# A fused Mamba and mixture-of-experts layer on one core: more identity products at the start, one mixer product ahead of the router's, one small step on another engine, and a new planned order

## The chip, the cores and the metric

The kernel runs on one core of a Trainium2 chip. The core has five engines with a queue of instructions each: TensorE (PE, matrix products; its weight loads are shown as PEld), VectorE (DVE), ScalarE (ACT), GpSimd (POOL) and SyncE (SP, which here only starts DMA transfers). Each engine takes its own instructions strictly in the order in which the program lists them; between engines semaphores pass the word that something is done. The metric is the device time of one execution in microseconds. Before the change three executions took 1305.14, 1308.02 and 1309.28 us, with a median of 1308.02 us.

## The reference

The input x has 16 batches of 256 positions and 256 features, all in float32. Each batch is normalised (layer norm without weights) and goes through two branches, whose results are added to x.

```python
def _L0_attn_ref(input_states, W_in, conv_kernel, conv_bias, W_x, W_dt, b_dt, W_out, A_log, D):
    proj = jnp.einsum('blh,he->bel', input_states, W_in)       # 256 -> 2 x 512 features
    hidden, gate = jnp.split(proj, 2, axis=1)
    x = lax.conv_general_dilated(hidden, conv_kernel, ...)     # 4 taps along the positions
    hidden = jax.nn.silu(x + conv_bias[None, :, None])
    hs_ble = hidden.transpose(0, 2, 1)
    ssm_p = jnp.einsum('ble,ed->bld', hs_ble, W_x)
    dt, Bm, Cm = jnp.split(ssm_p, [TR, TR + N], axis=-1)       # 128, 16, 16
    dts = jax.nn.softplus(jnp.einsum('blr,re->ble', dt, W_dt) + b_dt)
    dA = jnp.exp(dts[..., None] * A[None, None])               # 512 features x 16 states
    dBu = dts[..., None] * Bm[:, :, None, :] * hs_ble[..., None]
    ...                                                        # state = dA * state + dBu, y = sum over n of state * C
    y = (scan_out + hidden * D[None, :, None]) * jax.nn.silu(gate)
    return jnp.einsum('bel,eh->blh', y, W_out)

def _L0_ffn_ref(hidden_states, router_w, w_gate, w_up, w_down):
    probs = jax.nn.softmax(x @ router_w.T)                     # 32 experts
    rw, sel = jax.lax.top_k(probs, 8)                          # 8 of them kept, weights normalised
    ...                                                        # per expert e: acc += w_e * ((silu(x @ wg) * (x @ wu)) @ wd)

x = x + _L0_attn_ref(xn, ...) + _L0_ffn_ref(xn, ...)
```

All 32 experts (96 inner features each, 3072 together) are computed for every position; an expert that was not chosen has weight zero.

## The kernel before, in words

**Tiles and work of one batch.** A batch's x is loaded as one tile `xt` (`load_x`, L250). VectorE takes mean and variance (`stats`, L357), ScalarE the root (`root`, L367), VectorE the reciprocal (`invert`, L372), GpSimd the product minus mean times reciprocal in two tiny instructions (`center`, L378), and ScalarE normalises in place (`norm`, L385). TensorE turns the result (`turn`, L393), ScalarE copies it out of the accumulator memory as `xnT` (`keep_turned`, L401). Everything after that reads `xnT`:

- The router: `route` (L406) multiplies by the router's weights, VectorE, ScalarE and VectorE again make the eight largest weights (`largest`, `expo`, `choose`), SP writes them to DRAM (`send_weights`, L456, four transfers), and `spread` (L467, six transfers for each quarter of the experts) reads them back repeated over the partitions as `wr`, in a ring of two buffers.
- The experts, in 12 pairs q of column blocks: `gates` (two pairs at once, tiles pg), `silu` (tiles sg, ring of three), `weigh` on GpSimd (sg times wr, L509), `ups` (tiles pu), `combine` on VectorE (h = pu times sg, L513, ring of two), `down` (acc grows by h times the down weights, L525).
- The mixer: `project` (L531, two halves q of two column blocks, tiles ph), the convolution as `conv_first` on ScalarE (L542) and three taps `conv_rest` on VectorE (L554), `activate`, then `params`, `keep_params`, `send_params` (B and C to DRAM as bcd) and `widen`, `steps` (the step sizes dts), `skip`, `inputs`. The scan runs in 8 groups g of two states: `fetch` reads B and C of a group back over all partitions (tile rep, ring of three, L637), `feed` on GpSimd makes B times u (tile bu, L649), `decay` on ScalarE exponentiates (da, L663), `scan` and `read` on VectorE (L671, L683), and `collect` lets a DMA of GpSimd's queue add the product to y (L688). At the end `gate`, `gate_silu`, `fold`, `gated`, `project_out`, `finish`, `settle`, `store`.

**What sets the order.** The order on every engine is written by a planner at build time (class `Plan`, L20): each step is given an engine, a planned length, a due time, what it needs, and which slots of buffer rings it takes and gives back. `Plan.order` plays the steps through, and whenever an engine is free it takes the ready step with the earliest due time whose rings have room. The due time of a step is a base time of its batch (ORIGIN plus the batch's number times PERIOD, or RATE for the experts) plus an offset by kind of step from the tables DUE, and for the first, second and last batch also from FIRST, SECOND and LAST (`add`, L770). `early` holds a step back until its due time minus that. The planner's result is only an order: on the chip the engines run freely along it.

**DMA.** SP starts all loads from its one queue, in order. ScalarE's queue starts five small loads (`small`, L266 to L274) at the beginning. These transfers share eight completion semaphores, numbered 0 to 7, in rotation: a transfer that comes to a semaphore again first waits until the transfer before it on that semaphore has landed. The five small loads hold numbers 0 (conv kernel), 2 (conv bias), 4, 6 and 7, so SP's first three loads hold 1, 3 and 5, and from its fourth on SP goes through 0, 1, 2 and so on. In the order before, SP's first loads are x, router weights, first half of W_in, then W_x (number 0), W_dt (1), x again for the residual (2), and the first quarter of the expert weights.

**The start.** `warm` (L347) lets TensorE turn the identity 14 times from the moment it exists, `keep_warm` (L352) 6 times more after the router's weights were turned, and 4 times after the first `turn`.

Of the kernel before, what the change touches and what calls it, by code (L numbers as in the profile page):

```python
# [13 lines left out]
ALU = mybir.AluOpType  # L14
# [106 lines left out]
def mamba_moe_kernel(  # L121
# [30 lines left out]
    nc = tc.nc  # L152
# [26 lines left out]
    ORIGIN = -7.2  # L179
    PERIOD = 79.1  # L180
    RATE = 79.0

    DUE = dict(
        load_x=-300.5, stats=-15.5, root=132.5, invert=-162.0, center=-75.0, norm=244.0,
        turn=-535.0, keep_turned=-94.0, route=-100.0, largest=-231.5, expo=221.0, choose=-1192.5,
        send_weights=-260.5, project=-51.5, conv_first=455.5, conv_rest=185.0, activate=-293.5,
        params=-209.0, keep_params=-266.0, send_params=-303.5, widen=-273.0, steps=-79.0,
        skip=120.0, inputs=-299.5, fetch=-252.5, feed=315.5, decay=-34.0, scan=539.0, read=55.9,
        collect=-257.0, spread=65.5, gates=-25.5, ups=669.0, silu=245.5, weigh=233.0,
        combine=-138.5, down=288.0, settle=-496.5, gate=50.5, gate_silu=216.0, fold=502.5,  # L190
        gated=894.5, project_out=-81.0, load_again=-68.0, finish=160.0,
    )
    EARLY = dict(
        load_x=175.0, load_experts=25.0, stats=37.0, turn=1.0, route=277.0, project=671.0,
# [3 lines left out]
        route=179.5, largest=36.5, expo=-163.5, choose=655.5, project=409.0, conv_first=-563.0,  # L198
        conv_rest=-561.0, activate=218.5, params=-266.5, keep_params=285.0, widen=-51.5,
        steps=971.5, skip=-377.0, inputs=295.0, fetch=-161.5, feed=-360.0, decay=-135.0, scan=36.5,  # L200
        read=33.0, collect=-157.0, spread=-263.5, gates=-97.5, ups=-247.0, silu=-204.0,
        weigh=270.0, combine=402.0, down=53.0,
# [3 lines left out]
        load_x=-132.5, stats=-1.0, root=-131.0, invert=-137.5, center=-86.0, norm=251.0,  # L206
        turn=267.0, keep_turned=-305.5, route=89.0, largest=-27.5, expo=-14.0, choose=46.0,
        send_weights=8.0, project=267.5, conv_first=36.5, conv_rest=-36.5, activate=-61.0,
        params=26.0, keep_params=178.5, send_params=13.0, widen=126.5, steps=-25.0, skip=225.5,
        inputs=-138.5, fetch=-56.0, feed=24.0, decay=7.0, scan=104.0, read=31.5, collect=-154.0,  # L210
        spread=8.0, gates=1.5, ups=-251.0, silu=46.5, weigh=-137.5, combine=48.0, down=100.5,
        settle=-112.0, gate=-10.0, gate_silu=-83.0, fold=99.0, gated=-152.0, project_out=-44.0,
        load_again=-35.0, finish=22.5,
# [3 lines left out]
        fetch=-123.0, feed=-25.0, decay=359.0, scan=571.0, read=-65.0, collect=-281.5,  # L217
        spread=-131.0, gates=216.5, ups=75.5, silu=445.0, weigh=-274.5, combine=448.0, down=296.5,
        settle=-10.0, gate=-75.5, gate_silu=105.5, fold=-115.5, gated=339.0, project_out=-460.5,
        finish=479.0,  # L220
    )
    LEAD = -28.0
# [14 lines left out]
        rep=3, bu=3, pr=4, da=AHEAD, g=2, u=2, acc=1, wr=2, sg=3, h=2, gs=2, o=1,  # L237
# [140 lines left out]
    def center(b):  # L378
        mv, rstd = live["st", b]
        nmr = p1.tile([P, SPS, 1], F32, tag="nmr", name=f"nmr_{b}")  # L380
        nc.gpsimd.tensor_mul(nmr, mv[:, :, 0:1], rstd)
        nc.gpsimd.tensor_scalar(nmr, nmr, -1.0, None, ALU.mult)
        live["st", b] = rstd, nmr
# [382 lines left out]
    b = 0  # L766
    MM = 0.432
    KB = 1 / 280

    def add(kind, key, engine, length, due, *args, early=None, **kw):  # L770
        fn = kw.pop("fn", None) or steps_of[kind]
        if early is None:
            early = EARLY.get(kind, 1e9)
        due += DUE.get(kind, 0.0) + (FIRST.get(kind, 0.0) if b == 0 else 0.0)
        due += SECOND.get(kind, 0.0) if b == 1 else 0.0
        due += LAST.get(kind, 0.0) if b == B - 1 else 0.0
        plan.add((kind, *key), engine, length, due, fn, *args, early=early, **kw)

    steps_of = dict(
        load_x=load_x, stats=stats, root=root, invert=invert, norm=norm, turn=turn,  # L780
        keep_turned=keep_turned, route=route, largest=largest, expo=expo, choose=choose,
        project=project, conv_first=conv_first, conv_rest=conv_rest, activate=activate,
        params=params, keep_params=keep_params, widen=widen, steps=steps, skip=skip, inputs=inputs,
        fetch=fetch, spread=spread, gates=gates, ups=expand, silu=silu, combine=combine,
        weigh=weigh, down=down, settle=settle, gate=gate, gate_silu=gate_silu, gated=gated,
# [7 lines left out]
    add("keep_warm", (1,), "PE", 1.3, -490.0, 6, needs=[("turn_router",)])  # L793
    add("keep_warm", (2,), "PE", 0.8, -490.0, 4, needs=[("turn", 0)], gives=["warm"])
# [12 lines left out]
    for b in range(B):  # L807
        t = ORIGIN + PERIOD * b
        last = [] if b else [("load_in", 0)]
        x = ("x", b)  # L810
# [7 lines left out]
        add("center", (b,), "POOL", 0.15, t, b, needs=[("invert", b)], gives=[("mv", b)])  # L818
# [3 lines left out]
        add("turn", (b,), "PE", 1.0, t, b, needs=[("norm", b)], gives=[x],  # L822
# [3 lines left out]
        add("route", (b,), "PE", 0.9, t if b else t + 30.0, b, needs=[("keep_turned", b), ("keep_router",)],  # L826
# [4 lines left out]
        add("choose", (b,), "DVE", 1.35, t, b, needs=[("expo", b)], gives=[("pl", b)])  # L831
# [3 lines left out]
        for q in range(2):  # L835
            add("project", (b, q), "PE", 4 * MM, t, b, q, needs=[("keep_turned", b)] + last + ([("project", b, 0)] if q else []),
                takes=[("gu"[q], ("ph", b, q))] + ([] if q else [("hs", hs)]), gives=[xT])
            add("conv_first", (b, q), "ACT", 0.92, t, b, q, gives=[("ph", b, q)],
                needs=[("project", b, q)] + ([("conv_first", b, 0)] if q else []))
            add("conv_rest", (b, q), "DVE", 2.4, t, b, q,  # L840
                needs=[("conv_first", b, q)], gives=[("ph", b, q)])
# [20 lines left out]
        for g in range(GROUPS):  # L862
            at = t + PERIOD / GROUPS * g
            add("fetch", (b, g), "SP", 512 * KB, at, b, g, needs=[("send_params", b)],
                takes=[("rep", ("rep", b, g))], lands=5.5, early=14.0)
# [32 lines left out]
        for i in range(PARTS):  # L898
            add("spread", (b, i), "SP", 3.0, e + RATE / PARTS * i, b, i,
                needs=[("send_weights", b)], takes=[("wr", ("wr", b, i))], lands=6.0, early=20.0)  # L900
        for i in range(PAIRS // BATCH):
# [21 lines left out]
        add("load_again", (b,), "SP", 256 * KB, t, b, takes=[("o", ("o", b))], lands=8.0, early=25.0)  # L923
# [5 lines left out]
            needs=[("keep_turned", b)] + ([] if b else [("load_in", 1)]), early=10.0)  # L929
# [10 lines left out]
        for q in range(PAIRED):  # L940
# [8 lines left out]
            lands=7.0)  # L949
# [33 lines left out]
```

## Time and profile before

| what | value |
|---|---|
| times of three executions | 1305.14, 1308.02, 1309.28 us |
| the profiled execution, span | 1309.5 us, mean granted TensorE clock 0.993 |
| PE busy | 1288.9 us (98%), 5978 matrix instructions |
| PEld busy | 1109.9 us (85%) |
| DVE, ACT, POOL busy | 1157.5 (88%), 1133.9 (87%), 1181.6 us (90%) |
| DMA | 268.80 MB, mean 205 GB/s |
| chain of work that ended last | PE 63%, POOL 12%, DVE 8%, issue 6%, DMA 5%, ACT 4% |
| instructions by row | warm 128x128 transposes x24; ACT_TABLE_LOAD 1283 ns each; weigh (L509) x192, mean 1922 ns; feed (L649) x256, mean 2924 ns |

The times of the table are those of one profiled execution of 1309.5 us, 1.5 us above the median of the three timed ones. A busy TensorE is not the same as a TensorE at its full pace, because matrix instructions are pipelined and their ends are modelled; how many of them fall into a stretch tells more. All five engines are busy for 85% and more, so an instruction that one engine takes late is soon felt by the others.

### The profile page before, as it was taken

What the parts mean: (1) busy time and instruction counts of PE and PEld (TensorE: products, weight loads), DVE (VectorE), ACT (ScalarE), POOL (GpSimd) and SP (SyncE); (2) the same over time, 40 slices, a digit from 0 to 9 for tenths busy, and PEclk for the clock granted to TensorE, in tenths of its full rate; (3) what the DMA queues carried; (4) which work ended last, traced back from release to release, by engine and by line L of the source; (5) the groups of instructions that cost most, each with busy time, mean ns of one, the idle gap of its engine ahead of it and who ended that gap; (6) DMA issues with size and microseconds to landing.
All of it is one profiled execution on the core that took longest, in us unless ns stands there. A gap on an engine that the chain in (4) does not pass through costs nothing.

```text
span 1309.5 us, 18902 instructions
## 1 busy us (share of the span) xinstructions
PE 1288.9 (98%) x5978; PEld 1109.9 (85%) x5978; DVE 1157.5 (88%) x1719; ACT 1133.9 (87%) x1898; POOL 1181.6 (90%) x835
## 2 busy tenths in 40 slices
PE   9979999999999999999999999999999999999998
PEld 7868888887888888888888888888888888888887
DVE  3778989999899998989899898898989899899986
ACT  5878898997989989899898989989899898998883
POOL 1778999999999989999999898999999989998995
PEclk8999999999999999999999999999999999999999
DMA  9998899899999989999998988989899989998994
GB/s 248 241 230 191 189 237 195 215 206 211 201 222 198 226 199 200 199 212 206 199 215 188 213 191 206 225 189 209 185 216 216 197 193 203 217 210 193 202 221 94
DMA packets 169940, 268.80 MB, mean 205 GB/s; under 512 B 37840, under 2 KB 103920, under 8 KB 169840
## 3 DMA queue, kind: packets, MB, share of 16 engines
q0 software_dynamic: 36576, 124.80, 50.4%
q1 hardware_dynamic: 130624, 142.75, 40.4%
q8 instruction: 47, 0.77, 0.2%
q10 hardware_dynamic: 2640, 0.05, 0.1%
q14 instruction: 53, 0.43, 0.1%
HBM read 137.51 MB, written 5.24 MB: 109 GB/s over the span
## 4 chain that ended last, share of the span: by engine, by line
PE 63%; POOL 12%; DVE 8%; issue 6%; DMA 5%; ACT 4%; SPq 1%; POOLq 0%; DVEq 0%; ACTq 0%
PE acc L525 16%; PE pg L490 16%; PE pu L490 16%; POOL bu L649 6%; POOL sg L509 4%; PE px L574 3%; PE po L742 3%; PE ph L536 3%; DVE da L671 3%; PE pgate L716 3%; DMA y<-pr 2%; POOL y L688 2%; DVE hs L559 2%; DVE pr L683 2%; ACT da L663 2%
## 5 line engine op out<-in xcount | busy, mean ns | idle before, releaser
L649 POOL TENSOR_TENSOR bu<-rep,hs 128x1024 f32<-128x1024 f32 x256 | 716.4, 2924 | 59.7 <-DMA rep<-bcd 34.2
L671 DVE TENSOR_TENSOR_SCAN da<-da,bu 128x512 f32<-128x512 f32 x512 | 609.0, 1217 | 53.0 <-ACT da L663 44.8
L663 ACT ACTIVATE da<-dts,a_sb 128x256 f32<-128x256 f32 x1024 | 469.6, 473 | 84.6 <-DVE pr L683 61.9
L490 PE MATMUL pu<-xnT,wu_sb 128*128 128x256 f32 x1536 | 362.5, 382 | 5.8 <-DVE h L513 5.5
L525 PE MATMUL acc<-wd_sb,h 128*128 128x256 f32 x1536 | 364.2, 380 | 3.9 <-DVE h L513 3.8
L490 PE MATMUL pg<-xnT,wg_sb 128*128 128x256 f32 x1536 | 348.8, 380 | 3.1 <-DVE hs L559 1.5
L490 PEld LDWEIGHTS pu<-xnT,wu_sb 128*128 128x128 f32 x1536 | 292.6, 191 | 48.0 <-DVE h L513 7.5
L490 PEld LDWEIGHTS pg<-xnT,wg_sb 128*128 128x128 f32 x1536 | 291.0, 190 | 46.1 <-ACT sg L503 2.9
L525 PEld LDWEIGHTS acc<-wd_sb,h 128*128 128x128 f32 x1536 | 291.6, 190 | 45.1 <-DVE h L513 5.1
L509 POOL TENSOR_TENSOR sg<-sg,wr 128x512 f32<-128x512 f32 x192 | 326.3, 1922 | 2.3 <-ACT sg L503 2.3
L688 POOL DMA_DIRECT2D y<-pr x222 | 299.9, 1352 | 16.6 <-DVE da L671 5.8
L683 DVE TENSOR_TENSOR pr<-da,rep 128x512 f32<-128x512 f32 x448 | 294.0, 676 | 2.7 <-DVE pr L683 0.7
L663 ACT ACT_TABLE_LOAD x151 | 193.7, 1283 | 2.6
L513 DVE TENSOR_TENSOR h<-pu,sg 128x512 f32<-128x512 f32 x192 | 131.1, 683 | 58.9 <-POOL sg L509 31.8
L503 ACT ACTIVATE sg<-pg 128x512 f32<-128x512 f32 x192 | 105.3, 594 | 4.3 <-PE pg L490 2.1
L503 ACT ACT_TABLE_LOAD x81 | 103.9, 1283 | 2.9 <-PE pg L490 1.5
L732 POOL TENSOR_TENSOR y<-y,gs 128x512 f32<-128x512 f32 x30 | 79.4, 2816 | 0.2
L559 DVE SCALAR_TENSOR_TENSOR hs<-ph,small,hs 128x255 f32<-128x255 f32 (+2 forms) x192 | 76.0, 471 | 1.9 <-ACT hs L548 1.9
L707 POOL TENSOR_TENSOR y<-y 128x512 f32<-128x512 f32 x32 | 64.6, 2347 | 0.5 <-DMA y<-pr 0.5
L536 PE MATMUL ph<-xnT,win_sb 128*128 128x256 f32 x256 | 63.4, 392 | 0.0
L742 PE MATMUL po<-wout_sb,y 128*128 128x256 f32 x256 | 60.8, 380 | 1.0 <-DVE hs L559 1.0
L574 PE MATMUL px<-hs,wx_sb 128*32 128x256 f32 (+1 forms) x256 | 61.4, 387 | 0.0
(66 smaller groups left out, 863.4 us busy)
## 6 DMA issues: line engine op xcount, KB each, us to landing
y<-pr POOLq DMA_DIRECT2D x222, 512.0 KB, 7.0
rep<-bcd SPq DMA_DIRECT2D x128, 512.0 KB, 6.6
wr<-wd SPq DMA_DIRECT2D x128, 192.0 KB, 6.6
wr<-wd SPq DMA_DIRECT2D x128, 128.0 KB, 7.1
wr<-wd SPq DMA_DIRECT2D x128, 64.0 KB, 6.7
y<-sk POOLq DMA_DIRECT2D x32, 256.0 KB, 8.1
xt<-L_attn_input_states_dram SPq DMA_DIRECT2D x16, 256.0 KB, 4.9
o<-L_attn_input_states_dram SPq DMA_DIRECT2D x16, 256.0 KB, 6.9
```

The costliest lines, as they stand in the source:

```text
L490: nc.tensor.matmul(p[:, j, :], w[:, hc, ts(c, P)], xs[:, hc, :], start=(hc == 0), stop=(hc == HC - 1),)
L503: nc.scalar.activation(sg, live.pop(("g", b, q)), AF.Silu)
L509: nc.gpsimd.tensor_mul(sg, sg, wr[:, r : r + 2, :])
L513: nc.vector.tensor_mul(h, live.pop(("u", b, q)), live.pop(("sg", b, q)))
L525: nc.tensor.matmul(acc[:, s, :], h[:, j, ts(s, P)], wd_sb[:, c, :], start=(c == 0 and s == 0), stop=(c == FC - 1), skip_group_check=True,)
L536: nc.tensor.matmul(ph[:, j, :], win_sb[:, hc, ts(2 * q + j, P)], xs[:, hc, :], start=(hc == 0), stop=(hc == HC - 1),)
L559: nc.vector.scalar_tensor_tensor(cv[:, c, k:], ph[:, j, : L - k], cw[:, c, KC - 1 - k : KC - k], cv[:, c, k:], op0=ALU.mult, op1=ALU.add,)
L649: nc.gpsimd.tensor_mul(bu, live["rep", b, g][:, 0:1].to_broadcast([P, CPU, NG, L]), live["hs", b][:, ts(u, CPU), :].unsqueeze(2).to_broadc ...
L663: nc.scalar.activation(da[:, i, :], dts[:, c, :], AF.Exp, scale=a_sb[:, c, n : n + 1])
L671: nc.vector.tensor_tensor_scan(flat, flat, live["bu", k][:, j].rearrange("p n l -> p (n l)"), 0.0, op0=ALU.mult, op1=ALU.add,)
L683: nc.vector.tensor_mul(live["pr", k][:, :, j, :], live.pop(("da", m)), live["rep", b, g][:, 1])
L688: nc.gpsimd.dma_start(live["y", b, u].rearrange("p n c l -> p (n c l)"), live.pop(("pr", k)).rearrange("p n c l -> p (n c l)"), accum_op=A ...
```

## The change

The change does five things.

1. `keep_warm` turns the identity 20 times (before 6) after the router's weights, and 8 times (before 4) after the first turn.
2. In the first batch `center` is one VectorE instruction instead of two of GpSimd.
3. In the first batch `route` needs `project` half 0, and `project` half 1 needs `route`, so that the first half of the mixer's products stands ahead of the router's.
4. Planned lengths of some steps are others (turn 0.46, choose 1.8, center 0.74, store's landing 5.0), and `early` of fetch, spread, load_again and gate moves into the table EARLY.
5. All offsets, and ORIGIN, PERIOD, RATE and LEAD, are new, so the whole order is another one.

```diff
-    ORIGIN = -7.2
-    PERIOD = 79.1
-    RATE = 79.0
+    ORIGIN = -17.15
+    PERIOD = 78.78
+    RATE = 78.24
...
     EARLY = dict(
-        load_x=175.0, load_experts=25.0, stats=37.0, turn=1.0, route=277.0, project=671.0,
+        fetch=821.9, gate=647.5, load_again=320.0, load_experts=822.6, load_x=762.1,
+        project=2406.4, route=954.4, spread=434.4, stats=32.0, turn=628.4,
     )
...
-    LEAD = -28.0
+    LEAD = -26.74
...
-        nc.gpsimd.tensor_mul(nmr, mv[:, :, 0:1], rstd)
-        nc.gpsimd.tensor_scalar(nmr, nmr, -1.0, None, ALU.mult)
+        if b == 0:
+            nc.vector.scalar_tensor_tensor(
+                nmr, mv[:, :, 0:1], -1.0, rstd, op0=ALU.mult, op1=ALU.mult
+            )
+        else:
+            nc.gpsimd.tensor_mul(nmr, mv[:, :, 0:1], rstd)
+            nc.gpsimd.tensor_scalar(nmr, nmr, -1.0, None, ALU.mult)
...
-    add("keep_warm", (1,), "PE", 1.3, -490.0, 6, needs=[("turn_router",)])
-    add("keep_warm", (2,), "PE", 0.8, -490.0, 4, needs=[("turn", 0)], gives=["warm"])
+    add("keep_warm", (1,), "PE", 2.3, -490.0, 20, needs=[("turn_router",)])
+    add("keep_warm", (2,), "PE", 0.9, -490.0, 8, needs=[("turn", 0)], gives=["warm"])
...
-        add("center", (b,), "POOL", 0.15, t, b, needs=[("invert", b)], gives=[("mv", b)])
+        add("center", (b,), "POOL" if b else "DVE", 0.74 if b else 0.2, t, b, needs=[("invert", b)], gives=[("mv", b)])
...
-        add("route", (b,), "PE", 0.9, t if b else t + 30.0, b, needs=[("keep_turned", b), ("keep_router",)],
+        add("route", (b,), "PE", 0.9, t if b else t + 30.0, b, needs=[("keep_turned", b), ("keep_router",)] + ([] if b else [("project", b, 0)]),
...
-            add("project", (b, q), "PE", 4 * MM, t, b, q, needs=[("keep_turned", b)] + last + ([("project", b, 0)] if q else []),
+            add("project", (b, q), "PE", 4 * MM, t, b, q, needs=[("keep_turned", b)] + last + ([("project", b, 0)] if q else []) + ([] if b or not q else [("route", b)]),
...
-                takes=[("rep", ("rep", b, g))], lands=5.5, early=14.0)
+                takes=[("rep", ("rep", b, g))], lands=5.5)
```

What the new order is can be read from the two built programs, engine by engine. The steps that matter here:

- SP starts with the router's weights, then x, x again for the residual, W_x, W_dt, W_in's first half, W_in's second half (before: after the third quarter's down weights), the first quarter of the gate weights, the second batch's x, the first up and down weights, W_out (before: much later), and only then `send_weights`. Further on it lists the third quarter of `wr` ahead of the first three `fetch`, and the last quarter of `wr` ahead of the fourth.
- PE: identity x14, router turn, identity x20, turn of x, identity x8, project half 0, route, project half 1, pu 0, pg 0, pg 1, pu 1, params, pg 2, pg 3, turn of the second batch, then the first `down`.
- DVE in the first batch: both halves of `conv_rest` ahead of `choose` (before: behind it).
- ACT: `keep_router` ahead of the first `root`; the first table load for `expo` behind both halves of `conv_first`; 303 table loads in all instead of 311.
- POOL in the first batch: `weigh` of the pairs 8 and 9 ahead of both `feed` of group 4, of the pairs 10 and 11 between the two of group 5 (before: pair 8 behind group 4, pairs 9 to 11 behind group 5).

## The prediction

> **What bounds the kernel now.** First the busy time by stage, with the counts of matrix instructions (columns: stage, length, then busy us and count for PE, PEld, DVE, ACT and POOL, the granted clock, DMA share and GB/s):
>
> ```profile
> 10.70:90.00 79.30, 74.76 (x328) 61.63 (x329) 52.13 (x100) 59.77 (x102) 44.08 (x31) 0.96 0.96 252
> 90.00:170.00 80.00, 76.26 (x341) 64.34 (x340) 69.51 (x104) 68.14 (x117) 74.58 (x53) 0.96 0.88 192
> ...
> 250.00:330.00 80.00, 77.80 (x363) 66.48 (x363) 73.60 (x111) 69.28 (x118) 76.51 (x55) 1.00 0.92 206
> ...
> 650.00:730.00 80.00, 80.00 (x377) 69.45 (x376) 72.92 (x109) 72.21 (x120) 74.50 (x53) 1.00 0.92 202
> ...
> 1130.00:1210.00 80.00, 78.63 (x364) 66.63 (x363) 74.87 (x112) 68.83 (x121) 74.95 (x53) 1.00 0.90 206
> ```
>
> From 650 to 730 us TensorE never waits: 377 instructions in 80 us, 0.2122 us each. That is its pace, and no order makes it faster. What an order can win is what the other stages lose against it: 79.3 - 328 x 0.2122 = 9.7 us up to 90, 80 - 341 x 0.2122 = 7.6 us up to 170, 3.0 us from 250 to 330 and 2.8 us from 1130 to 1210 in the same way, besides 10.7 us before the first mixer product. POOL is busy for 74.5 of 80 us there, so an order has little room on it.
>
> Then the start in order of time, with what SP's queue waited for (start, duration, engine, line, operation; the two last rows are from the list of waits):
>
> ```profile
> 1.37 3.07 PE L354 MATMUL warm<-ident 128*128 128x128 f32 x14 [1.37 <-POOL eps_sb L318]
> ...
> 4.61 0.64 PEld L354 LDWEIGHTS warm<-ident 128*128 128x128 f32 x6
> ...
> 6.41 0.37 SPq L749 DMA_DIRECT2D o<-L_attn_input_states_dram  x1
> ...
> 7.86 0.87 PEld L354 LDWEIGHTS warm<-ident 128*128 128x128 f32 x4
> ...
> 10.68 5.51 PE L536 MATMUL ph<-xnT,win_sb 128*128 128x256 f32 x16
> ...
> 13.43 0.24 DVE L451 STREAM_TRANSPOSE wT<-rest 128x64 f32<-128x64 f32 x1
> ...
> 19.99 8.10 SPq L476 DMA_DIRECT2D wr<-wd  x12
> ...
> 27.31 2.50 POOL L509 TENSOR_TENSOR sg<-sg,wr 128x512 f32<-128x512 f32 x2
> ...
> 31.31 1.89 PE L525 MATMUL acc<-wd_sb,h 128*128 128x256 f32 x8
> ```
> ```profile
> SPq L288 <- DMA small<-_L_attn_conv_kernel_dram: 1.9, 1, 1.9
> ...
> SPq L749 <- DMA small<-in_L_attn_conv_bias_dram: 1.4, 1, 1.4
> ```
>
> The reader is to see two chains. SP's fourth and sixth load go out only at 4.11 and 6.41, when small loads of ScalarE's queue have landed. And the router's result (wT at 13.67) takes until 27.3 to come back as wr, on which the first weigh, h and down hang.
>
> Last the ramp, where TensorE stands still and its clock is halved after it (the last two rows are again by stage, here PE busy and count, clock, DMA share, GB/s):
>
> ```profile
> 74.00 4.65 POOL L649 TENSOR_TENSOR bu<-rep,hs 128x1024 f32<-128x1024 f32 x2 [7.54 <-DMA rep<-bcd]
> ...
> 81.30 2.51 PE L525 MATMUL acc<-wd_sb,h 128*128 128x256 f32 x8 [2.83 <-DVE h L513]
> ...
> 96.97 3.78 PE L490 MATMUL pu<-xnT,wu_sb 128*128 128x256 f32 x8 [3.08 <-DVE h L513]
> ```
> ```profile
> 84.00:85.00 1.00, 1.00 (x4) 0.50 0.67 133
> ...
> 98.00:99.00 1.00, 1.00 (x4) 0.50 1.00 246
> ```
>
> **Identity products.** 18 more. By the weight loads six took 0.64 us (0.107 each) and four, later, at clock 0.50, 0.87 (0.217). The 20 so take 2.1 us from about 4.7, until 6.8, within the idle time before the turn at 6.94; at the slow pace 4.3 us, and the turn is 2.1 us late. The 8 take 0.9 or 1.7 us beside the copy of xnT (8.31 to 8.90). I take the fast pace, nearest to the row that they follow, and nothing on the path.
>
> The granted clock fell to 0.50 at 7.25 us, after the gap from 5.49 to 6.94, and came back at about 14.6, four us into real products. Yet identity products did raise the pace before: the first 14 weight loads took 2.83 us (0.20 each), the six next 0.107 each. [...]
>
> **Center on VectorE and x second in the queue.** Before, POOL's pair lay between the reciprocal's end at 5.67 and norm at 6.29; one instruction of 0.17 to 0.23 us (the reciprocal 128x2 and the SCALAR_TENSOR_TENSOR of 128x64) with 0.1 of handover saves some 0.3 us. But x goes out at 1.23 instead of 0.74, of which 0.2 vanish in root's wait for the table load until 5.19. Sum 0, between -0.2 and +0.3.
>
> **W_in sixth in SP's queue.** It takes the place of o: semaphore 2, free at 6.41, where before it went out at 1.73. From issue to landing its 512 KB took 4.5 us then; W_x, 320 KB, took 3.7. So it lands between 10.1 and 10.9, against xnT at 8.9: project half 0 starts about when it did (10.68). The half product ahead of the router's gains the mixer the route's 1.7 us, and the wait for W_in eats it.
>
> **The router's chain.** Route now follows project half 0, and choose follows both halves of conv_rest. At full clock: half 0 from 10.5 to 12.2, route to 13.1, half 1 to 14.8, conv_first to 15.9, conv_rest (4.76 us for both) to 18.4, choose (1.91 us, 11.76 to 13.67 before) to 20.3. At half clock 2.0 us later, 22.4. Against 13.67 that is 6.7 to 8.7 late. Behind wT the queue is the same as before: four sends (2.58), two quarters' loads (3.6), six wr. The sixth wr went out at 22.9 and took 4.2, so it landed at 27.1; now at 33.8 to 35.8. From there to h's end it took 2.2 us (29.3), which gives 36 to 38, and 0.3 more to the down. TensorE's work up to the first down is the same before and after (route, ten groups and a turn, 18.5 us by 1.7 a group); it reached it at 31.31 with h waiting since 29.3. The loss is 36.3 - 31.3 = 5 to 38.3 - 31.3 = 7 us; I take 6. Nothing covers it: sg has three slots, so the fourth silu waits for this h, and behind it on ACT stand xnT of the second batch and dts, and so all decays. After an idle stretch of 3.1 us (93.9 to 97.0) the clock stood at 0.50 for 6.6 us and cost half of that; after one of 2.8 us (78.5 to 81.3) for 3.8. So 2 us more, between 0 and 3.3. **Plus 8, between 5 and 10.3.**
>
> **The ramp.** The halt at 78.5 has its cause at 74.00: rep of group 3, issued at 61.92, took 12 us behind 3.6 MB of weights. The new order lists it ahead of the last up and down weights, and half of W_in and W_out (1 MB, 3.7 us at the 283 GB/s of 70 to 80 us) have gone early. I take that halt as gone: 2.8 us and 1.9 of clock. The halt at 94 (0.9 before it, 3.1, and 3.3 of clock: 7.3) hung on weigh 9 behind the feeds of groups 4 and 5, which it now precedes; against it, the first three fetches now stand behind a wr that waits for weigh 2, and the first feed starts at some 48 instead of 41.8. I leave it where it is. **Minus 4.7, between 0 and -12.**
>
> **The middle.** How far the first down of a pair stands behind its gates, in PE work (1.7 us for each group of 8), can be counted in both orders. Before, the least distance in a batch is 13.6 us or more but for batches 0, 1, 3 and 14 (11.9, 10.2, 10.2, 8.5); 3 and 14 are the two stages with 3.0 and 2.8 us lost. After, both are repaired (13.6 and 15.3), but batches 7, 9 and 10 have 8.5, 10.2 and 8.5, and 5 and 15 have 11.9. At 2.9 us each that is minus 5.8 and plus 8.7, and up to 5.8 for the mild ones. **Plus 3, between -5.8 and +8.7.** The eight table loads less (1.283 us each) lie on ACT, busy for 72 of 80 us and not what TensorE waits for: nothing.
>
> **Sum.** 8 - 4.7 + 3 = +6.3 on the profile's 1309.5, which is 1315.8; the median of the runs lies 1.5 below the profile, so 1314 as a time. Full sums of the bounds: 5 - 12 - 5.8 = -13 (1295) and 10.3 + 0 + 8.7 = +19 (1327).
>
> **The rivals.** *The ramp pays for the start* (faster): both halts of the ramp vanish with their half clock, -12, the late router costs 6 without a clock penalty, and the middle is even: 1308 - 6 = 1302; with the middle repaired 1296. For it: DMA was the limit from 60 to 80 us (1.07 to 1.12 share), which a delay of TensorE does not lengthen, and POOL weighs earlier. Against it: wr of the third quarter blocks SP's queue ahead of the fetches. *Even*: the halts gone, the start at its full 8 and the middle +3: 1307. *The middle breaks* (slower, more): POOL, busy 93%, lets all five near batches wait, 14.5 - 5.8 = 8.7 more, with the ramp unchanged: 8 + 8.7 = +17, 1325; it decides from the point where weigh is done later than its gates plus 8.5 us. *The clock does not hold* (the change doesn't do what it says): route and half 1 late by 2 us, the upper end of the router's term, 1315.
>
> **How the numbers follow.** Forecast, with its clock variant, 0.35 (1310 to 1319 alone); the middle breaks 0.12; even 0.17; ramp pays 0.36. What differs by under 0.3% (3.9 us) from before can't be told from no change. So slower 0.47, same 0.17, faster 0.36. The range runs from 1299 to 1325: it leaves out the lower part of the ramp's case and the upper part of the last.
>
> **What would show it.** W_in issued at about 6.4 and project half 0 at 10 to 11; wT at 20 to 22; the first down at 36 to 38 with a wait for h; a granted clock of 1.00 from 8 to 14 if the identities hold it. No wait of POOL for rep near 74. Full stages (377 in 80 us) where batches 3 and 14 stood, and fewer where 7, 9 and 10 stand. I am wrong if by 110 us more matrix instructions are done than the 428 of before and the 18 new ones, or if the stages from 550 to 1050 stay full.

## The result, and the profile after

| | median | lowest to highest | executions |
|---|---|---|---|
| before | 1308.16 us | 1304.36 to 1310.98 | 20 |
| after | 1312.96 us | 1305.35 to 1319.62 | 20 |

The changed kernel is slower by a ratio of 1.0034, 95% interval [1.0022, 1.0047], which is 4.4 us (2.9 to 6.1). Its times also spread twice as far: half of them lie between 1310.7 and 1315.2 us.

One caution ahead of the profile. The profiled execution has a span of 1306.4 us and a time of 1308.16, 4.8 us below the median of its kernel. By the same distance of 1.76 us, the profiled execution of before (span 1309.5) took some 1311.3, 3.1 above its median. So the two profiles stand in the wrong order. They show where work waits; what that costs is read from the repeated runs.

First the start of the kernel after the change, from the timeline (start, duration, engine, line, operation, count; in brackets the idle time before and what ended it):

```profile
4.45 0.88 SPq L281 DMA_DIRECT2D win_sb<-in_L_attn_W_in_dram  x2
...
4.90 3.59 PE L375 MATMUL warm<-ident 128*128 128x128 f32 x20
8.32 0.60 PE L424 MATMUL pt<-ident,xt 128*128 128x128 f32 x4
...
10.10 1.97 PE L562 MATMUL ph<-xnT,win_sb 128*128 128x256 f32 x8 [0.30 <-DMA win_sb<-in_L_attn_W_in_dram]
11.90 0.97 PE L439 MATMUL pl<-rwT,xnT 128*128 128x32 f32 x8
...
15.68 0.67 PE L516 MATMUL pu<-xnT,wu_sb 128*128 128x256 f32 x2 [0.99 <-DMA wu_sb<-in_L_ffn_w_up_dram]
...
19.79 0.25 DVE L477 STREAM_TRANSPOSE wT<-rest 128x64 f32<-128x64 f32 x1
...
25.49 3.84 PE L600 MATMUL px<-hs,wx_sb 128*32 128x256 f32 x16 [1.90 <-ACT sg L529]
...
26.98 7.28 SPq L502 DMA_DIRECT2D wr<-wd  x12
...
33.01 3.72 POOL L535 TENSOR_TENSOR sg<-sg,wr 128x512 f32<-128x512 f32 x3 [9.48 <-DMA wr<-wd]
...
35.05 0.66 PE L424 MATMUL pt<-ident,xt 128*128 128x128 f32 x4 [2.26 <-DVE h L539]
35.54 1.89 PE L551 MATMUL acc<-wd_sb,h 128*128 128x256 f32 x8
```

The whole chain of the router has moved: wT at 19.79 (before 13.43), the first weigh at 33.01 (27.31), the first down at 35.54 (31.31), and TensorE stands still for 2.26 us ahead of the turn of the second batch. That wait for h is not all of it. TensorE had waited 0.99 and 0.42 us for the first up weights and 1.90 us for ScalarE's first silu, which the new order lists behind the skip products and the second batch's root (24.84, before 22.64); before, its one wait between the first product and the first down was 0.19 us. Without the wait for h the first down would have come at about 33.3, still 2.0 us later than before.

Then TensorE by stage (stage, length, PE busy and number of matrix instructions, granted clock, DMA share, GB/s), and the one halt of the ramp that is left:

```profile
10.70:90.00 79.30, 73.72 (x346) 1.00 0.96 258
90.00:170.00 80.00, 76.55 (x351) 0.98 0.86 193
...
570.00:650.00 80.00, 78.19 (x367) 1.00 0.86 192
730.00:810.00 80.00, 77.94 (x363) 1.00 0.90 204
810.00:890.00 80.00, 79.03 (x368) 1.00 0.88 201
1050.00:1130.00 80.00, 80.00 (x377) 1.00 0.90 206
1130.00:1210.00 80.00, 80.00 (x376) 1.00 0.90 204
```
```profile
112.31 2.89 PE L551 MATMUL acc<-wd_sb,h 128*128 128x256 f32 x8 [2.87 <-DVE h L539]
```

In this pair of executions the ramp does more: 697 instructions from 10.7 to 170 us against 669, and the halts at 78 and 94 us are gone. But the 669 are the lowest of four profiles of the old ramp; in the three kernels below that keep it whole (old start, small parts, new end) the same stretch has 687, 698 and 685, and in the second execution of the changed kernel 691. So the counts show no gain of the ramp. In the middle the three stages 570 to 650, 730 to 810 and 810 to 890 have 1098 instructions where before had 3 x 377; 33 x 0.2122 is 7.0 us lost. The same stages before:

```profile
570.00:650.00 80.00, 80.00 (x377) 1.00 0.92 205
730.00:810.00 80.00, 80.00 (x377) 1.00 0.91 203
810.00:890.00 80.00, 80.00 (x377) 1.00 0.90 202
```

From 1050 to 1210 it is 753 against 736, 3.6 us won. Over all stages from 170 to 1290 us, 5221 stand against 5228: the rest of the order as a whole loses 1.5 us in this execution.

### The profile page after: what moved, and what is told of

It is laid out like the page before. It is cut to its first block, busy times and chain, and to the rows that moved or that the text cites. A ratio compares the mean times of both kernels' runs of the same rounds, so it can differ in the third digit from the quotient of the medians.

```text
span 1306.4 us, 18935 instructions
## 1 busy us (share of the span) xinstructions
PE 1285.2 (98%) x5996; PEld 1108.0 (85%) x5996; DVE 1158.5 (89%) x1720; ACT 1121.6 (86%) x1890; POOL 1182.0 (90%) x833
## 4 chain that ended last, share of the span: by engine, by line
PE 69%; POOL 9%; DVE 6%; DMA 6%; ACT 4%; issue 4%; SPq 2%; POOLq 0%; ACTq 0%; DVEq 0%
PE acc L551 18%; PE pu L516 18%; PE pg L516 17%; POOL bu L675 4%; PE po L768 4%; PE px L600 4%; PE pgate L742 3%; PE ph L562 3%; DMA rep<-bcd 3%; POOL sg L535 2%; DVE da L697 2%; PE pdt L623 2%; DVE hs L585 2%; ACT da L689 1%; POOL y L714 1%
## 5 line engine op out<-in xcount | busy, mean ns | idle before, releaser
L675 POOL TENSOR_TENSOR bu<-rep,hs 128x1024 f32<-128x1024 f32 x256 | 702.5, 2863 | 48.5 <-DVE da L697 28.3
L535 POOL TENSOR_TENSOR sg<-sg,wr 128x512 f32<-128x512 f32 x192 | 306.5, 1832 | 12.3 <-DMA wr<-wd 9.7
L714 POOL DMA_DIRECT2D y<-pr x222 | 291.8, 1324 | 17.0 <-DVE da L697 6.0
L733 POOL TENSOR_TENSOR y<-y 128x512 f32<-128x512 f32 x32 | 68.6, 2268 | 0.0
L758 POOL TENSOR_TENSOR y<-y,gs 128x512 f32<-128x512 f32 x30 | 60.0, 2123 | 0.7
```

Source lines behind the costliest of these rows:

```text
L535: nc.gpsimd.tensor_mul(sg, sg, wr[:, r : r + 2, :])
L675: nc.gpsimd.tensor_mul(bu, live["rep", b, g][:, 0:1].to_broadcast([P, CPU, NG, L]), live["hs", b][:, ts(u, CPU), :].unsqueeze(2).to_broadc ...
L714: nc.gpsimd.dma_start(live["y", b, u].rearrange("p n c l -> p (n c l)"), live.pop(("pr", k)).rearrange("p n c l -> p (n c l)"), accum_op=A ...
```

## The experiments

The theory to be tested: the late router chain in the start and the near downs of batches 7, 9 and 10 each cost some us, and a calmer ramp and a better end pay part of it back. The rivals: the start costs through the gap before W_in and the halved clock, not through the router; or all the loss is in the middle.

Each ratio is against runs of the kernel before on the same chip and in the same sitting: 35 runs (median 1308.28) for the four kernels of the first part, 20 (1307.60) for the router ahead, W_in third, few identities and the mended start, 21 (1307.88) for the other four.

### Where the loss lies: four kernels

In kernels joined of two orders, `plan_new()` and `plan_old()` give the planned steps of after and before, and `follow` takes so many steps of the first and then what is left in the order of the second.

**The changed kernel again.** No edit.

> The changed kernel once more, for a second profile on the chip of the next three runs. Its first profile spans 1306.4 us, 6.5 below its median time, so that profile cannot show all of the loss. Theory 1 (the order's middle costs): 1309 to 1316 us as a time, and a profile longer than the first shows its extra waits from 550 us on. Theory 2 (the start costs): the same time, and the extra waits lie before 170 us, with the granted clock at 0.50 for some us there.

1312.15 us, ratio 1.0031 [1.0016, 1.0046]. The loss stands. Its profiled execution (span 1308.4, again below the median) differs from the one above in a way that explains a part of the spread. From its timeline:

```profile
4.89 2.40 PE L375 MATMUL warm<-ident 128*128 128x128 f32 x20
...
10.04 1.96 PE L562 MATMUL ph<-xnT,win_sb 128*128 128x256 f32 x8 [1.39 <-DMA win_sb<-in_L_attn_W_in_dram]
...
34.75 0.66 PE L424 MATMUL pt<-ident,xt 128*128 128x128 f32 x4 [2.03 <-DVE h L539]
35.24 3.23 PE L551 MATMUL acc<-wd_sb,h 128*128 128x256 f32 x8
```

The same 20 identities took 2.40 us instead of 3.59, and the projection still began at 10.04: it waits for W_in. And here the clock fell behind the wait for h, and the first down took 3.23 us instead of 1.89 (granted clock 0.62 from 36 to 40 us, 1.00 in the other execution).

**The new order for the start and ramp only**, some 165 us, and the old order behind.

```diff
...
-    plan.issue()
+    order = follow(plan_new(), 445, plan_old())
+    for st in order:
+        st["fn"](*st["args"])
```

> The new order for its first 445 steps (up to about 165 us), the old order for all others. Theory 1 (the middle of the new order costs, its start gains): faster than before by about 4.5 us, the 21 matrix instructions that the first profile was ahead at 180 us: 1303 to 1304. Theory 2 (the start costs on most executions): 1311 to 1314, as the changed kernel. Stages from 330 to 1050 full (377 in 80 us) by both.

1314.35 us (1308.14 to 1322.13), ratio 1.0044 [1.0023, 1.0066]. Its profiled execution is one of the long ones (span 1318.5). From the timeline:

```profile
10.39 3.00 PE L497 MATMUL ph<-xnT,win_sb 128*128 128x256 f32 x8 [1.97 <-DMA win_sb<-in_L_attn_W_in_dram]
13.19 1.76 PE L374 MATMUL pl<-rwT,xnT 128*128 128x32 f32 x8
...
38.36 4.94 POOL L470 TENSOR_TENSOR sg<-sg,wr 128x512 f32<-128x512 f32 x4 [11.24 <-DMA wr<-wd]
40.40 1.11 PE L359 MATMUL pt<-ident,xt 128*128 128x128 f32 x4 [4.02 <-DVE h L474]
41.31 3.62 PE L486 MATMUL acc<-wd_sb,h 128*128 128x256 f32 x8
```

Here the wait for W_in was 1.97 us, the clock fell to 0.50 behind it, and route took 1.76 instead of 0.97; wT came at 23.42, the first down at 41.31, 10 us behind the old order's, and again at half clock. So the new start has a long tail, and the 1303 to 1304 of the first theory did not come. The join itself costs something too: 359 instructions from 170 to 250 us, where both orders have 372 and more (13 x 0.2122 = 2.8 us).

**The old start and ramp, the new order behind.** The first term of the mean is back on POOL and the identities are 6 and 4.

```diff
...
-    plan.issue()
+    order = follow(plan_old(), 442, plan_new())
+    for st in order:
+        st["fn"](*st["args"])
```

> The old order and the old start for the first 442 steps, the new order for all others. Theory 1: slower than before by the middle's waits, 2.1 + 3.0 + 1.9 + 0.9 us where the first profile has them (570 to 650, 730 to 890, 330 to 410), less the 3.9 that the old order loses from 1050 to 1210: +4 to +8, 1312 to 1316. Theory 2: as before, 1306 to 1310.

1310.84 us, ratio 1.0019 [1.0007, 1.0032], between the two expectations: 2.5 us (0.9 to 4.2) for all that lies behind 165 us. The same three stages are short here (367, 361 and 365 instructions), so they do not come from the start. What is left for the start and ramp is 0.0034 - 0.0019, some 2 us, with wide bounds.

**The old order with the new start's small parts**: identities 20 and 8, and the first mean term on VectorE.

```diff
-    add("keep_warm", (1,), "PE", 1.3, -490.0, 6, needs=[("turn_router",)])
-    add("keep_warm", (2,), "PE", 0.8, -490.0, 4, needs=[("turn", 0)], gives=["warm"])
+    add("keep_warm", (1,), "PE", 1.3, -490.0, 20, needs=[("turn_router",)])
+    add("keep_warm", (2,), "PE", 0.8, -490.0, 8, needs=[("turn", 0)], gives=["warm"])
...
-        nc.gpsimd.tensor_mul(nmr, mv[:, :, 0:1], rstd)
-        nc.gpsimd.tensor_scalar(nmr, nmr, -1.0, None, ALU.mult)
+        if b == 0:
+            nc.vector.scalar_tensor_tensor(
+                nmr, mv[:, :, 0:1], -1.0, rstd, op0=ALU.mult, op1=ALU.mult
+            )
...
```

> The old order; only the identity products are 20 and 8 instead of 6 and 4, and the first mean term is on VectorE. If the identities hold the clock: granted 1.00 from 7 to 15 us, the mixer's first products done 2 us earlier, the time 1 to 3 us below before, 1305 to 1307. If they do not count for the clock (rival): granted 0.50 from about 7 us on as before, 20 products of 0.217 us, the turn 2 us late, 1308 to 1310.

1307.65 us, ratio 0.9992 [0.9982, 1.0001], between the two expectations. These parts do no harm; alone they are worth between nothing and 2.4 us. TensorE by stage, first the kernel before, then this one (same columns as above):

```profile
7.00:10.00 3.00, 2.84 (x13) 0.59 1.03 297
10.00:14.00 4.00, 4.00 (x13) 0.50 1.15 305
```
```profile
7.00:10.00 3.00, 3.00 (x28) 1.00 1.12 352
10.00:14.00 4.00, 4.00 (x23) 1.00 1.12 314
```

The clock was 1.00 where it was 0.50. That the identities did this is not shown, for the kernel with the old start and the new order behind has 6 and 4 of them, as before, and its profiled execution kept 1.00 as well:

```profile
7.00:10.00 3.00, 2.60 (x19) 1.00 1.08 335
10.00:14.00 4.00, 4.00 (x20) 1.00 0.87 226
```

There TensorE had stood still for 0.69 us before the first turn, in the kernel before for 1.46 us; so the clock there differs from execution to execution. The first down came at 29.32 here, at 30.66 with the old start and at 31.31 in the kernel before.

### What in the start: the router, W_in or the identities

Four kernels with one change each to the changed kernel. `ahead(names, of)` moves steps in the planned order in front of another.

**The router's chain ahead.**

```diff
...
+    order = ahead([("route", 0)], ("project", 0, 0))
+    order = ahead([("largest", 0), ("expo", 0), ("choose", 0), ("send_weights", 0)], ("conv_first", 0, 0))
...
```

> The changed kernel with the router's chain put back ahead: route stands before the first half of the first projection, and largest, exponential, choice and the sends before the first half of the convolution. Theory A (the late router chain is what the start costs, about 4 us up to the first down): wT at 13 to 15 us, the last word of wr at 27 to 29, the first down at 30 to 32 with no wait of PE for h over 0.5 us, and a time of 1305 to 1309. Rival B (the gap in which PE waits for W_in, and the clock that it costs in some executions, is the cause): the same chain comes early, but the time stays at 1310 to 1313.

1309.77 us (1308.47 to 1312.09), ratio 1.0015 [1.0002, 1.0027]. That is 2.5 us better than the changed kernel (0.0034 - 0.0015; by the two intervals between near 0 and some 5 us) and 0.8 us above what theory A gave, while B's 1310 to 1313 is missed too. The spread has gone with it: 3.6 us over 11 runs. The timeline shows why the first down did not come at 30 to 32:

```profile
13.14 0.24 DVE L477 STREAM_TRANSPOSE wT<-rest 128x64 f32<-128x64 f32 x1
...
15.63 0.67 PE L516 MATMUL pu<-xnT,wu_sb 128*128 128x256 f32 x2 [1.51 <-DMA wu_sb<-in_L_ffn_w_up_dram]
...
17.41 2.45 SPq L325 DMA_DIRECT2D wg_sb<-in_L_ffn_w_gate_dram  x2
19.91 4.56 SPq L325 DMA_DIRECT2D wu_sb<-in_L_ffn_w_up_dram  x2
24.57 7.28 SPq L502 DMA_DIRECT2D wr<-wd  x12
...
30.41 4.96 POOL L535 TENSOR_TENSOR sg<-sg,wr 128x512 f32<-128x512 f32 x4 [6.40 <-DMA wr<-wd]
...
33.55 1.89 PE L551 MATMUL acc<-wd_sb,h 128*128 128x256 f32 x8
...
87.51 6.95 POOL L675 TENSOR_TENSOR bu<-rep,hs 128x1024 f32<-128x1024 f32 x3 [7.26 <-DMA rep<-bcd]
93.46 2.07 PE L623 MATMUL pdt<-dt,wdt_sb 128*128 128x256 f32 x4 [4.14 <-DVE h L539]
```

wT is 6.65 us earlier, but the weight loads that the new order lists ahead of wr keep SP until 24.57, so wr goes out only 2.4 us earlier. The first down comes 2.0 us earlier, and here it is TensorE's own work that comes late to it: h is ready at 32.40, and TensorE reaches the turn at 33.11 without a wait. It had waited 1.51 and 0.47 us for the first up weights, and behind that the clock was 0.50 from 18 to 20 us, so that the two gates took 4.58 us instead of 3.69. And a halt of the ramp is back: POOL's feed at 87.5 had waited 7.26 us for rep, and TensorE stands for 4.14 us before 93.5. That the earlier start is what made rep late was not tested by itself.

**W_in third in the queue.**

```diff
...
+    order = ahead([("load_in", 0)], ("load_again", 0))
...
```

> The changed kernel with the two copies of W_in third in SP's queue instead of sixth; nothing else is moved. Rival B (gap and clock): W_in lands at 6.2 to 7.0 us, the first half of the projection starts at 7.7 to 8.9 right behind the turned x, the granted clock is 1.00 from 10 to 18 us, and the time is 1306 to 1309 with a narrower spread. Theory A (the late router chain): wT moves only to about 18 to 19, the first down to about 34, and the time is 1309 to 1311.5.

1313.7 us, ratio 1.0043 [1.0030, 1.0056]. The first half went out at 1.65, the second still waited for its semaphore until 5.46; the projection began at 9.61 with no wait. wT came at 19.29 and the first down at 34.89, and the time did not fall. So taking the wait for W_in away brought nothing, against rival B; theory A's small gain was not seen either. The steady clock that B asked for was had only until 17 us: it fell to 0.50 behind waits of 1.34 and 0.37 us for the up weights, and again behind a wait of 1.99 us for h.

**Few identities**, 6 and 4 in the new order.

```diff
-    add("keep_warm", (1,), "PE", 2.3, -490.0, 20, needs=[("turn_router",)])
-    add("keep_warm", (2,), "PE", 0.9, -490.0, 8, needs=[("turn", 0)], gives=["warm"])
+    add("keep_warm", (1,), "PE", 2.3, -490.0, 6, needs=[("turn_router",)])
+    add("keep_warm", (2,), "PE", 0.9, -490.0, 4, needs=[("turn", 0)], gives=["warm"])
```

> The changed kernel with 6 and 4 identity turns ahead of the two turned tiles instead of 20 and 8. Rival B (the clock in the start decides): the clock is 0.50 from about 7 to 15 us as before the change, wT at 21.5 to 22.5, the first down at 37 to 38, and the time is 1314 to 1316. Rival C (the identities only delay the turned x, by up to 1.4 us, and the clock is worth little behind them): wT at 19 to 20, the first down at 35, and the time is 1311 to 1313.

1313.75 us, ratio 1.0052 [1.0038, 1.0066]. The path is nearly B's: half clock behind a wait of 1.81 us for W_in (the first half of the projection took 3.62 us), wT at 21.30, the first down at 36.83. The time lies between the two expectations, some 2.5 us above the changed kernel, with intervals that overlap. In the new order the extra identities do not hurt, and probably help.

**The first mean term back on POOL**, the changed kernel otherwise.

```diff
-        if b == 0:
-            nc.vector.scalar_tensor_tensor(
-                nmr, mv[:, :, 0:1], -1.0, rstd, op0=ALU.mult, op1=ALU.mult
-            )
-        else:
-            nc.gpsimd.tensor_mul(nmr, mv[:, :, 0:1], rstd)
-            nc.gpsimd.tensor_scalar(nmr, nmr, -1.0, None, ALU.mult)
+        nc.gpsimd.tensor_mul(nmr, mv[:, :, 0:1], rstd)
+        nc.gpsimd.tensor_scalar(nmr, nmr, -1.0, None, ALU.mult)
```

> The changed kernel with the first mean term back on POOL, in two instructions; nothing else. Theory (the term lies behind W_in, which arrives later than the turned x anyway): norm 0.3 to 0.4 us later, the first half of the projection unchanged, 1311.5 to 1313.5. Rival (the second gap before the turn tips the clock): 1314 or more.

1314.33 us, ratio 1.0048 [1.0029, 1.0067]. The median lies in the rival's range and above the theory's, but it is not to be told from the changed kernel's 1.0034 [1.0022, 1.0047], and six runs do not settle a term this small. In the profiled execution the projection began at 9.81, so nothing was lost on its way to W_in, and the clock stayed at 1.00 until the wait for h at 34 us, so the rival's mechanism was not seen.

### The middle and the end

**A mended start with the old order behind.** Router ahead, W_in third, and from step 445 on the old order.

```diff
...
+    order = follow(plan_new(), 445, plan_old())
+    order = ahead([("route", 0)], ("project", 0, 0))
+    order = ahead([("largest", 0), ("expo", 0), ("choose", 0), ("send_weights", 0)], ("conv_first", 0, 0))
+    order = ahead([("load_in", 0)], ("load_again", 0))
...
```

> The first 445 planned steps (up to about 165 us) as in the changed kernel but with the router's chain ahead and W_in third, all later steps in the order of before. If start and middle are both what the change lost, and its ramp without the halts at 78 and 94 us is a gain that stays: first down at 30 to 32, no stretch at 0.83 between 70 and 100 us, the middle as before, and a time of 1298 to 1304, under both kernels. Rival (the halts of the ramp depend on the start and return when it is early, so that nothing is gained): a stretch at 0.83 before 130 us, and a time of 1305 to 1309.

1310.68 us, ratio 1.0023 [1.0011, 1.0035]. The hope is refuted and the rival's mechanism is seen: POOL waited 8.0 us for rep in the ramp, and the stretch from 90 to 100 us had 27 instructions at a clock of 0.83. The time is above the rival's as well; part of that is the join, which left 365 instructions from 170 to 250 us.

**The old order for the middle**, from about 450 to 1010 us.

```diff
...
+    order = plan_new()
+    held = [st for st in order[:1172] if st["name"] != ("gates", 4, 4)]
+    order = follow(follow(held, len(held), plan_old()), 2704, plan_new())
...
```

> The changed kernel with its planned order up to about 450 us and from about 1010 us on, and the order of before in between, where the new order has batches 7, 9 and 10 (570 to 650, 730 to 890 us). Theory (near downs after their gates lose time in these batches, 2.1 + 3.0 + 1.9 us by the counts of the profile after): 377 instructions in each of the stages 570:650, 730:810 and 810:890, and a time of 1305 to 1307.5. Rival (the loss there is made good again elsewhere, since POOL or the transfers set the pace over several batches): the three stages are full, but others lose as much, and the time stays at 1311 to 1313.

1309.79 us (1307.18 to 1315.83), ratio 1.0028 [1.0011, 1.0045]. By stage:

```profile
330.00:410.00 80.00, 77.81 (x363) 1.00 0.93 213
410.00:490.00 80.00, 78.75 (x369) 1.00 0.93 204
490.00:570.00 80.00, 78.79 (x369) 1.00 0.96 210
570.00:650.00 80.00, 80.00 (x377) 1.00 0.91 206
730.00:810.00 80.00, 80.00 (x377) 1.00 0.93 206
810.00:890.00 80.00, 80.00 (x377) 1.00 0.91 203
```

The three stages are full as expected, 7.0 us won. But around the join 363 + 369 + 369 stand against 373 + 376 + 376 of the changed kernel: 24 x 0.2122 = 5.1 us are given back. The expected time was missed for that reason. It shows where the changed kernel loses, not what a good plan would gain.

**The same with the router ahead.**

```diff
...
+    order = ahead([("route", 0)], ("project", 0, 0))
+    order = ahead([("largest", 0), ("expo", 0), ("choose", 0), ("send_weights", 0)], ("conv_first", 0, 0))
...
```

> The same, and the router's chain ahead again as in the run router_first. If the late chain (2.5 to 3 us) and the near downs (5.5 to 7 us) are two separate losses that add up: 1302 to 1304.5, under the kernel before. Rival (they share slack, so that one of them is hidden behind the other): no faster than the run old_middle by more than 1 us.

1308.43 us, ratio 1.0003 [0.9989, 1.0016]. As far as the expected 1302 it did not go, since the middle's gain was mostly eaten by the join. The router is worth another 1.4 us by the medians, 3.3 by the ratios. By the ratios the two losses do not hide one another, by the medians that is barely past the 1 us of the rival; with both taken out the time is that of before, the join included.

**The old order with the new end**, with the identities and mean term of the change.

```diff
...
+    order = follow(plan_old(), 2704, plan_new())
...
```

> The order of before up to its step 2704 (about 1010 us), the new order from there, with the 20 and 8 identity turns and the first mean term on VectorE. Theory (batch 14, which lost 2.8 us in the profile before, is repaired by the new order): 376 or 377 instructions from 1130 to 1210 us, and a time of 1304 to 1306, against 1307.65 for the order of before with the same start. Rival (what batch 14 loses is taken up by slack at the end): 1307 to 1308.

1302.42 us (1300.81 to 1304.63), ratio 0.9959 [0.9942, 0.9975]: better than both kernels and than the 1304 to 1306 expected, by 5.4 us against before and by 4.3 us (0.9992 - 0.9959) against the old order with the small parts. The last stages, first of the old order with the small parts, then of this kernel:

```profile
1050.00:1130.00 80.00, 78.95 (x369) 1.00 0.91 202
1130.00:1210.00 80.00, 77.64 (x360) 1.00 0.91 202
1210.00:1290.00 80.00, 79.25 (x365) 1.00 0.93 200
```
```profile
1050.00:1130.00 80.00, 80.00 (x377) 1.00 0.91 203
1130.00:1210.00 80.00, 80.00 (x376) 1.00 0.90 203
1210.00:1290.00 80.00, 80.00 (x373) 1.00 0.88 196
```

32 instructions more, 6.8 us, in the same 240 us (one execution each; the kernel before had 1107 there, 19 fewer than this one), and TensorE waits for nothing from 1050 us on. The end of the new order is its one clear gain.

## Why the prediction came out as it did

The predicted 1314 stands against 1312.96, slower as forecast. By term:

- **Identity products**, nothing on the path: right in the sum. The fast pace was taken; 2.40 us came in one execution and 3.59 in another, which turned x at 8.32 instead of 6.94. Both were covered by W_in, as the prediction's cover said. That the larger number holds the clock is not shown, since the old start kept 1.00 with 6 and 4. But the pace did rise on transposes alone: the first 14 took 3.25 us (0.23 each), the next 20 in the second execution 0.12 each, and the first half of the projection, behind nothing but transposes, took 1.97 us in the changed kernel, against 3.62 at half clock with few identities.
- **Center on VectorE**, 0: not resolved. 0.16 us for the one instruction, and W_in later than the turned x anyway.
- **W_in sixth in SP's queue**: it went out at 4.45 instead of 6.41, because its semaphore came free earlier, but it took some 5.5 us to land instead of 4.5, so the projection began at 10.10, as predicted: two misses that offset each other. The variant that the clock does not hold was not only a rival: after a wait of 1.97 us for W_in it fell to 0.50, after 1.39 it did not.
- **The router's chain**, plus 8: the chain came late as described, the size was too large. wT 19.79 (20.3 to 22.4 predicted), wr used at 33.01 (33.8 to 35.8), first down 35.54 (36.3 to 38.3). That is 4.2 us late instead of 6, and the half clock behind it cost its part in one execution and nothing in the other. Taking the chain back brings 2.5 us. The prediction had TensorE's way to the first down the same before and after, and that was wrong: with its waits for the up weights and for silu it would have come 2.0 us later by itself, so only 2.26 of the 4.2 us hang on h. That is why the first down came no earlier than 33.55 with the router ahead.
- **The ramp**, minus 4.7: the halt at 78 is gone as predicted, the one at 94 too, which had been left in place, while one at 112 came. Here the sign came that the prediction had set against itself: by 110 us 484 matrix instructions were done (481 in the second execution), more than 428 + 18 = 446. Much of that lead is the draw of the two profiles. Against the execution with the old start, which has the 6 and 4 identities of before and 450 by 110 us, it is 484 - 18 - 450 = 16, and it does not last: the mark lies behind the halts of the old order and ahead of the new one, and by 170 us 726 and 720 without the 18 stand against 728. So the prediction's course up to 110 us, with one halt left in its place, was wrong, and by 170 us start and ramp together come out between even and 2 us lost in these executions. Start and ramp together were predicted as 8 - 4.7 = +3.3; the runs give some 2 (0.0034 less 0.0019), of which the router's place alone makes 2.5. No run has the ramp by itself: 2 less the 4.2 of the start, or less 6 with a halved clock behind it, leaves -2 to -4. The half clock behind the two halts before lasted 3.4 and 6.8 us by slices of 0.2 us, where the prediction reads 3.8 and 6.6, and the clock of the start fell at 7.6 and came back at 14.4 instead of 7.25 and 14.6; no term moves by more than 0.2 us for it.
- **The middle**, plus 3: measured 2.5 us [0.9, 4.2] with the old start. Batches 7, 9 and 10 lost 2.1, 3.0 and 1.9 us where 2.9 each was set, and the milder 5 and 15 next to nothing; batch 14 was repaired (364 to 376). Batch 3 was not (363 to 366 in its stage, one execution each), though its distance is as good: there the count of distances did not tell. The 2.5 us hold both signs: the end of the new order wins 4.3, so what lies between it and the ramp loses some 6.8, close to the 7.0 of the three stages. The wait is the one that was named; in the changed kernel's timeline:

```profile
610.57 1.99 PE L516 MATMUL pu<-xnT,wu_sb 128*128 128x256 f32 x8 [1.81 <-DVE h L539]
```

- **The rivals.** "The ramp pays for the start" was right about the halts and wrong about the sum: the profiled execution has no halt at 78 or 94 and still lies above 1302. "The middle breaks" did not come: of the five near batches three lost, and by less. "Even" had both halts gone and the start at its full size; its 1307 is 6 us too low.

So the middle came out nearly as it was worked out, while start and ramp were both set too large, with opposite signs, and TensorE's own waits in the start and the place of the new halt were not foreseen. That the total stayed right to 1 us is in part luck.

## What to carry to other kernels

Before a half product is put ahead of a chain that goes out to DRAM and back, count everything that this chain passes, and look at what stands ahead of its last step in the queue: putting the router 6.65 us earlier moved its result by only 2.4 us, since weight loads stood in front of it, and TensorE itself came no earlier than 33.55 us for the first down. A new order from a planner is a bundle of gains and losses: cut it where both orders have done the same steps and time the pieces, for the best kernel of this study is the old order with the new end. And an execution's profile is one draw: here the slower kernel's profile was the shorter one.

## What the runs showed that was not expected

- The clock fell after short gaps, and not always: TensorE stood for 2.26 us before the second batch's turn and kept 1.00, stood for 2.03 us there in another execution of the same kernel and fell to 0.50 for the three slices from 36 to 39 us; a gap of 1.39 us before the projection cost nothing, one of 1.97 at the same place, in the kernel with the new start only, was followed by half clock until about 18 us. With the router ahead, the clock was 0.50 from 18 to 20 us behind waits of 1.51 and 0.47 us with 0.67 us of work between them. Gaps of nearly the same length fared differently, so these runs show no length of gap that decides it.
- The spread of the times may follow such gaps. Half of the changed kernel's times lie in 4.5 us (20 runs, standard deviation 3.3); with the router ahead, where the gap before the first down is gone, the deviation is 1.2, and 1.35 in the old order with more identities. But the profiled execution with the router ahead has other gaps and two stretches at half clock, so this is a guess; that the gaps are the cause was not tested by itself.
- The pace of 20 identities at the same place was 0.12 us each in some executions (2.40 us for all in the second one of the changed kernel) and 0.18 in others (3.59 in the first one, with a granted clock shown as 1.00 in every slice up to 10 us).
- An earlier first down is not an earlier end: 2.0 us won at 30 us, by one profile each, left 1.0 us (nothing to 2.4) at the end, and with the router ahead a wait for rep came back in the ramp.
